# A graph network on one core: 340 stores of layer 0 issued from ScalarE's queue instead of SyncE's

## The chip, the core and the metric

The kernel runs on one NeuronCore of a Trainium2 chip. The core has TensorE (PE, matmuls; PEld are its weight loads), VectorE (DVE), ScalarE (ACT), GpSimd (POOL) and SyncE (SP). SP does no arithmetic here; it issues transfers. A transfer is an instruction in the queue of the engine that issues it, and 16 DMA engines then move the data. Each engine works its own queue in order, so an instruction that waits for a semaphore holds everything behind it on the same engine.

The metric is device time in microseconds for the whole program, one launch. Before the change it was 2840.71 us (median of three runs, 2832.33 to 2841.24).

## The reference

Two message-passing layers over a graph of 6250 nodes with 64 features and 206,250 edges sorted by target. Cut to what matters (LN is the layer norm):

```python
h = maximum(LN(x), 0)                                     # layer 0
msg = relu(h[src] + edge_attr_16 @ W_edge.T + b_edge)
h = (h + segment_sum(msg, dst)) @ W1.T + b1
x = x + relu(batch_norm(h)) @ W2.T + b2
h = maximum(LN(x), 0)                                     # layer 1
Y = relu(concat(h[src], edge_attr_64) @ M_W.T + M_b)
Z = segment_sum(Y, dst)
x = x + relu(concat(h, Z) @ U_W.T + U_b)
```

## The kernel before

**Groups and blocks.** Edges come in 101 groups of 16 tiles of 128 edges. The first 71 groups (targets of the low nodes) are sorted by their source's block: for each of 35 target blocks of 128 nodes the edges lie in a DRAM region `place` of 50 tiles, one tile for each source block and one for what overflows. DVE works out each edge's place (`places`, `rank`), POOL scatters the rows to `place` by 16 indirect transfers a group (L840), and SP fills the region with -1 beforehand (`fill_part`). The last 30 groups are not sorted: POOL gathers the source rows by indirect transfers (L545, class `Direct`).

**A step of a sorted block.** A block of 50 tiles is worked in seven steps of up to 8 tiles (`CH`, class `Sorted`). In layer 0 a step does this:

- `ahead` has SP load the block's rows `eb` (2050 KB, two buffers) and the next steps' source columns `st` (a row of DRAM `src_rows` spread over 128 partitions, six buffers). `columns`, once for each block, has PE transpose the column of sources, ACT writes it as `cols` (L331), and it is stored in `src_rows`; `sources` reads it back from there.
- `prepare`: PE transposes the 16 edge attributes, ACT copies them to `at` (L314), DVE compares `st` with the partition's number and so makes the 0/1 matrix `hot_s` (L434).
- `keep`: ACT casts `hot_s` to 8 bits, `hot_8` (L440, two buffers), and it is stored in DRAM `hots` for layer 1, which reads it in place of making it again.
- `gather`: PE multiplies `at` by the edge weights and `hot_s` by the node table's three parts `tab`; `messages`: ACT's relu to `msg` (L468); `targets`: DVE makes `hot_d` (L459); `sums`: PE multiplies `msg` by `hot_d` into the block's sum.

A `Direct` step of layer 0 makes the layer 1 edge terms as well: PE to `pe`, ACT copies them to `e1` (L611, two buffers), and they are stored in DRAM `terms`.

**What sets the order.** PE, DVE and ACT run in program order (`manual_schedule`). Every transfer that goes through the helper `load` (L139 to L142) is issued by SP and kept in program order, loads and stores alike: all have L141 in the profile. POOL's transfers are paced by `pace`: every other one waits for a matmul of the slot before. The two Line objects and `slot` interleave the steps of blocks with the sorting of later groups; a block's rows are loaded one slot before its `columns`.

**Semaphores of transfers.** In the built program the transfers of SP and ACT share eight completion semaphores, given out in turn in program order, and each transfer waits until the one eight places earlier has landed, unless its engine already knows that it has.

Of the kernel before, what the change touches and what calls it, by code (L numbers as in the profile page):

```python
# [37 lines left out]
F32 = mybir.dt.float32  # L38
# [8 lines left out]
P = 128  # L47
D = 64
# [31 lines left out]
def window(g):  # L80

    return min(max((g * GT * P * N // E - 31) // P, 0), SB - 2)
# [16 lines left out]
def gnn_kernel(  # L99
# [24 lines left out]
    nc = tc.nc  # L124
# [14 lines left out]
    def load(to, what):  # L139

        i = nc.sync.dma_start(to, what)  # L141
        return tc.keep_in_program_order(i) if in_order[0] else i  # L142
# [20 lines left out]
    def bank(shape, name, tag, bufs=1, dtype=F32):  # L163
        return ps.tile(shape, dtype, name=name, tag=tag, bufs=bufs)
# [157 lines left out]
    src_rows = dram.tile([SB, T * P], BF16, name="src_rows")  # L322
    hots = dram.tile([P, SB, T * P], F8, name="hots")

    def columns(layer, d, eb):

        if layer == 0:
            p = bank([T, P], "st_p", "tr")
            nc.tensor.transpose(p, eb[:, :, SRC], ident)
            cols = zero.tile([T, P], BF16, name="cols")  # L330
            nc.scalar.activation(cols, p, AF.Identity, bias=shift[:, d:d + 1])  # L331
            load(src_rows[d, :].rearrange("(t p) -> t p", p=P), cols)
        dl = work.tile([P, T, 1], F32, name="dl")
        nc.vector.tensor_scalar(dl[:, :, 0], eb[:, :, DST], float(-P * d), None, op0=OP.add)
        attrs = None
        if layer == 0:
            attrs = zero.tile([P, T, ED], F32, name="attrs")
            nc.scalar.copy(attrs, eb[:, :, D:D + ED])
        return dl, attrs
# [79 lines left out]
    class Sorted:  # L419
# [16 lines left out]
        def keep(self):  # L436

            n = self.n
            hot_8 = zero.tile([P, 8, P], F8, name="hot_8")
            nc.scalar.copy(hot_8[:, :n, :], self.hot_s[:, :n, :], saturate=False)  # L440
            load(hots[:, self.d, self.a * P:self.b * P],
                 hot_8[:, :n, :].rearrange("p t q -> p (t q)"))

        def gather(self):
            n, layer = self.n, self.layer
# [18 lines left out]
        def messages(self):  # L464
            n, gp = self.n, self.gp
            self.msg = msg = pools[self.layer].tile([P, 8, D], F32, name="msg", bufs=2 + self.layer)
            if self.layer == 0:
                nc.scalar.activation(msg[:, :n, :], gp[:, :n, :], AF.Relu)  # L468
            else:
                nc.vector.tensor_add(msg[:, :n, :], gp[:, :n, :], self.eb[:, self.a:self.b, 0:D])  # L470
                nc.scalar.activation(msg[:, :n, :], msg[:, :n, :], AF.Relu)  # L471
# [15 lines left out]
    class Blocks:  # L487
# [9 lines left out]
        def ahead(self):  # L497

            if self.i == len(self.list):
                return  # L500
            d, c = self.list[self.i]
            for b, from_c in ((d, 0), (d + 1, 1)):
                if b < SB and b not in self.rows and c >= from_c and self.age(b) >= 1:
                    self.rows[b] = self.load_rows(b)
            for b, from_c in ((d, 0), (d + 1, len(CH) - 1 if self.layer else 2)):
                if b in self.rows and b not in self.cols and c >= from_c and self.age(b) >= 2:
                    self.cols[b] = columns(self.layer, b, self.rows[b])
            there = self.rows if self.layer else self.cols
            for j in range(self.i, min(self.i + 6, len(self.list))):
                if j not in self.st and self.list[j][0] in there:  # L510
                    self.st[j] = sources(self.layer, *self.list[j])
# [39 lines left out]
    terms = dram.tile([ND, P, GT * D], F32, name="terms")  # L551
# [16 lines left out]
    class Direct:  # L568
# [30 lines left out]
        def messages(self):  # L599
            n = self.n  # L600
            half = slice(8 * self.h, 8 * self.h + n)
            if self.layer == 1:
                self.msg = self.gat[:, half, :]
                nc.vector.tensor_add(self.msg, self.msg, self.ea[:, half, :])
                nc.scalar.activation(self.msg, self.msg, AF.Relu)
                return
            self.msg = msg = zero.tile([P, 8, D], F32, name="msg")[:, :n, :]
            nc.vector.tensor_add(msg, self.pm[:, :n, :], self.gat[:, half, :])
            nc.scalar.activation(msg, msg, AF.Relu)
            e1 = self.pool.tile([P, 8, D], F32, name="e1", bufs=2)  # L610
            nc.scalar.copy(e1[:, :n, :], self.pe[:, :n, :])  # L611
            load(terms[self.g, :, 8 * self.h * D:(8 * self.h + n) * D],
                 e1[:, :n, :].rearrange("p t d -> p (t d)"))

        def sums(self):
# [77 lines left out]
    with tc.tile_pool(name="sort", bufs=1) as sort:  # L693
# [219 lines left out]
        for j0, j1 in chunks:  # L913
            n = j1 - j0
# [13 lines left out]
        with tc.manual_schedule(engines=ordered):  # L928
            for g in range(1, GS):
# [7 lines left out]
                d = window(g) + 3  # L937
# [34 lines left out]
    p = bank([P, P], "most_p", "tr")  # L972
# [69 lines left out]
    p = bank([P, P], "b2_p", "tr")  # L1042
# [59 lines left out]
    cols = [slice(a, min(a + 4 * P, NH * P)) for a in range(0, NH * P, 4 * P)]  # L1102
# [259 lines left out]
```

## Time and profile before

| what | value |
|---|---|
| median of three timed runs | 2840.71 us |
| profiled execution, its own time | 3512.69 us |
| span in the profile | 3510.9 us |
| mean granted TensorE clock | 0.767 |
| PE busy, share of the span | 63% |
| POOL busy | 59% |
| DVE busy | 48% |
| ACT busy | 24% |
| HBM moved | 538.24 MB, mean 153 GB/s |

The profiled execution took 3512.69 us, 24% over the median. Every duration and wait below is from that one execution, and a time worked out of it is brought to the timed runs by the factor 2840.71/3512.69 = 0.809, as a whole; the profile doesn't tell which of its stages were the longer for being recorded.

The stages can be told from where lines start and end: POOL's scatters (L840) run from 33 to 1817 us, its gathers for the last groups of layer 0 from 1823 us; the last `terms` store is issued at 2572 us; layer 1's first `st` load at 2632 us. In the rows of groups, a row gives line, engine, operation, tiles out<-in, count, then busy us and mean ns of one, then the engine's idle time just before these instructions and what ended most of it. "remote" there means a semaphore whose update the profile couldn't put down to an instruction. SPq and ACTq are the engines' queues; issuing a transfer isn't counted as busy.

### The profile page before, as it was taken

To read this page: it belongs to the slowest core of one execution; us is meant where nothing else is said; L and a number is where in the kernel's file an instruction comes from. 1 tells how busy PE (TensorE), PEld (TensorE's weight loads), DVE (VectorE), ACT (ScalarE), POOL (GpSimd) and SP (SyncE) were. 2 spreads that over 40 slices of the span, in tenths; PEclk is the share of its full clock that TensorE was granted. 3 is DMA by queue.
4 is the path that set the end of the run, shared out by engine and by line. 5 is a ranking of instruction groups with operands and counts; after the bars stand their busy time and mean duration, and the time that the engine had idled before them with its cause. 6 is when DMAs were issued, how large, how long until landed. Compare 5 with 4: busy or idle time off the path is not lost. (4 is left out here: it accounts for less than half of the span.)

```text
span 3510.9 us, 56266 instructions
## 1 busy us (share of the span) xinstructions
PE 2221.8 (63%) x20444; PEld 1666.0 (47%) x20444; DVE 1692.4 (48%) x3562; ACT 842.8 (24%) x1612; POOL 2060.9 (59%) x2098
## 2 busy tenths in 40 slices
PE   1336677677676766666675754444566767777777
PEld 1224455455454545444454533333345656565655
DVE  4725555455555545545442321121144656666667
ACT  1213233223233323223232210111131222222222
POOL 5666666666666666666665466666605455555552
PEclk7568877777778787778788876676677877878778
DMA  7747775766766776666644323232326545455553
GB/s 178 187 125 192 193 187 161 200 165 191 187 175 191 192 193 164 184 165 191 173 139 136 114 78 78 70 84 66 77 73 176 182 148 174 150 177 164 163 171 117
DMA packets 340180, 538.24 MB, mean 153 GB/s; under 512 B 114229, under 2 KB 245557, under 8 KB 330933
## 3 DMA queue, kind: packets, MB, share of 16 engines
q1 hardware_dynamic: 263972, 453.43, 45.5%
q0 software_dynamic: 66816, 79.02, 9.8%
q10 hardware_dynamic: 9104, 2.10, 0.4%
q8 instruction: 163, 2.67, 0.3%
q14 instruction: 125, 1.02, 0.1%
HBM read 358.81 MB, written 175.52 MB: 152 GB/s over the span
## 5 line engine op out<-in xcount | busy, mean ns | idle before, releaser
L840 POOL DMA_INDIRECT place<-to,ix x1136 | 1149.7, 1012 | 661.8 <-issue 284.2
L545 POOL DMA_INDIRECT gat<-table,src_d x952 | 903.2, 949 | 712.3 <-PE gp L148 213.7
L459 DVE TENSOR_TENSOR hot_d<-cbank,dl 128x1024 f32<-128x1024 f32 (+1 forms) x490 | 542.2, 1107 | 910.3 <-remote 332.5
L148 PE MATMUL pa<-hot_d,msg 128*64 128x128 f32 (+1 forms) x5250 | 859.0, 359 | 112.8 <-issue 91.6
L148 PEld LDWEIGHTS pa<-hot_d,msg 128*64 128x64 f32 (+1 forms) x5250 | 620.0, 182 | 237.1 <-issue 146.2
L148 PE MATMUL gp<-we,at 128*128 128x512 f32 (+1 forms) x490 | 290.9, 681 | 291.3 <-issue 167.8
L595 DVE TENSOR_TENSOR hot_d<-cbank,rel_d 128x1024 f32<-128x1024 f32 x120 | 145.7, 1214 | 504.7 <-remote 347.8
L148 PE MATMUL gp<-tab,st 128*128 128x64 bf16 x5250 | 258.4, 203 | 163.6 <-issue 146.1
L148 PEld LDWEIGHTS <-st 128*128 128x128 fp8e4 x5250 | 203.9, 104 | 235.4 <-issue 229.4
L148 PEld LDWEIGHTS <-hot_s 128*128 128x128 bf16 x5250 | 215.5, 106 | 182.9 <-issue 166.8
L471 ACT ACTIVATE msg<-msg 128x512 f32<-128x512 f32 (+1 forms) x245 | 143.0, 584 | 531.4 <-DVE msg L470 399.2
L314 ACT COPY at<-at_p 128x128 f32<-128x128 f32 (+1 forms) x245 | 64.9, 265 | 811.1 <-remote 478.3
L148 PE MATMUL gp<-tab,hot_s 128*128 128x64 bf16 x5250 | 229.5, 204 | 26.4 <-issue 21.8
L148 PEld LDWEIGHTS gp<-we,at 128*128 128x128 f32 (+1 forms) x490 | 90.9, 228 | 322.4 <-issue 184.1
L440 ACT CAST hot<-hot_s 128x1024 fp8e4<-128x1024 bf16 (+1 forms) x245 | 233.4, 953 | 43.2 <-DMA hots<-hot 18.9
L148 PE MATMUL pd<-hot_d,msg 128*128 128x256 f32 x476 | 149.8, 470 | 75.8 <-DVE acc L380 66.2
L470 DVE TENSOR_TENSOR msg<-gp,eb 128x512 f32<-128x512 f32 (+1 forms) x245 | 153.5, 627 | 90.9 <-remote 47.8
L148 PEld LDWEIGHTS pm<-we,ea 128*128 128x128 f32 x1136 | 175.6, 223 | 34.4 <-DMA ea<-in_ea 13.0
L148 PE MATMUL pm<-we,ea 128*128 128x128 f32 x1136 | 177.5, 307 | 20.8 <-DMA ea<-in_ea 13.1
L313 PE MATMUL at_p<-ident,attrs 128*128 128x128 f32 (+1 forms) x245 | 84.9, 347 | 140.8 <-issue 75.1
L148 PE MATMUL pe_d<-we,ea_d 128*128 128x128 f32 x476 | 85.3, 333 | 131.2 <-issue 60.5
L148 PEld LDWEIGHTS pe_d<-we,ea_d 128*128 128x128 f32 x476 | 78.2, 240 | 181.6 <-issue 94.7
(181 smaller groups left out, 2158.9 us busy)
## 6 DMA issues: line engine op xcount, KB each, us to landing
eb<-place SPq DMA_DIRECT2D x70, 2050.0 KB
place<-minus SPq DMA_DIRECT2D x175, 410.0 KB
st<-src_rows SPq DMA_DIRECT2D x210, 256.0 KB
ea<-in_ea SPq DMA_DIRECT2D x71, 512.0 KB
hots<-hot SPq DMA_DIRECT2D x210, 128.0 KB
st<-hots SPq DMA_DIRECT2D x210, 128.0 KB
place<-to,ix POOLq DMA_INDIRECT x1136
ea_d<-in_ea SPq DMA_DIRECT2D x30, 512.0 KB
```

The lines of the kernel that those rows point to most:

```text
L148: i = nc.tensor.matmul(*args, **kwargs)
L313: nc.tensor.transpose(p[:n * ED, :], attrs.rearrange("p t f -> p (t f)"), ident)
L314: nc.scalar.copy(at[:n * ED, :], p[:n * ED, :])
L440: nc.scalar.copy(hot_8[:, :n, :], self.hot_s[:, :n, :], saturate=False)
L459: nc.vector.tensor_tensor(self.hot_d[:, :n, :], slot_p[:, None, :].to_broadcast([P, n, P]), self.dl[:, self.a:self.b, :].to_broadcast([P, ...
L470: nc.vector.tensor_add(msg[:, :n, :], gp[:, :n, :], self.eb[:, self.a:self.b, 0:D])
L471: nc.scalar.activation(msg[:, :n, :], msg[:, :n, :], AF.Relu)
L545: i = nc.gpsimd.indirect_dma_start(out=gat[:, t, :], out_offset=None, in_=table, in_offset=bass.IndirectOffsetOnAxis(ap=src_d[:, k:k + 1], ...
L595: nc.vector.tensor_tensor(self.hot[:, :n, :], slot_p[:, None, :].to_broadcast([P, n, P]), rel_d[:, self.k:self.k + n, None].to_broadcast([ ...
L840: i = nc.gpsimd.indirect_dma_start(out=place[:, :], out_offset=bass.IndirectOffsetOnAxis(ap=ix[:, t:t + 1], axis=0), in_=to[:, t, :], in_o ...
```

## The change: three stores leave `load` for `nc.scalar.dma_start`

The stores of `cols` (35 of them, 12.5 KB each), `hot_8` (245, 128 KB each, 32 KB for a block's last) and `e1` (60, 256 KB, one of 128 KB) are issued by ACT, just behind the instruction that makes them. The 8-bit store is now described as 32-bit words, with the same bytes in each partition. Nothing else is edited.

```diff
@@ columns
-            load(src_rows[d, :].rearrange("(t p) -> t p", p=P), cols)
+            nc.scalar.dma_start(src_rows[d, :].rearrange("(t p) -> t p", p=P), cols)
@@ Sorted.keep
             nc.scalar.copy(hot_8[:, :n, :], self.hot_s[:, :n, :], saturate=False)
-            load(hots[:, self.d, self.a * P:self.b * P],
-                 hot_8[:, :n, :].rearrange("p t q -> p (t q)"))
+            nc.scalar.dma_start(hots[:, self.d, self.a * P:self.b * P].bitcast(F32),
+                                hot_8[:, :n, :].rearrange("p t q -> p (t q)").bitcast(F32))
@@ Direct.messages
             nc.scalar.copy(e1[:, :n, :], self.pe[:, :n, :])
-            load(terms[self.g, :, 8 * self.h * D:(8 * self.h + n) * D],
+            nc.scalar.dma_start(terms[self.g, :, 8 * self.h * D:(8 * self.h + n) * D],
                  e1[:, :n, :].rearrange("p t d -> p (t d)"))
```

In the built program PE's and POOL's order is the same as before, and DVE's but for two spots (one instruction some 60 places later, three neighbours exchanged). SP has 340 transfers fewer, ACT 340 more, each directly behind its L331, L440 or L611 and waiting for that instruction's end. 226 of the 340 also wait for the transfer eight places earlier to land; in 219 of these that one is SP's.

## The prediction, made before the changed kernel ran

> **What bounds the kernel now.** The waits of SP's own queue come first, since the change is about SP:
>
> ```profile
> SPq L141 <- ACT hot L440: 608.0, 114, 12.5
> SPq L141 <- ACT e L611: 206.5, 33, 26.3
> SPq L141 <- ACT cols L331: 84.9, 19, 44.0
> SPq L141 <- DMA src_rows<-cols: 39.5, 25, 3.3
> ```
>
> The columns are us in total, times, longest. SP stands 899 us (608.0 + 206.5 + 84.9) at the three stores, waiting for ACT to make what they store. The loads behind a store wait with it. Does anybody wait for those loads? The view of line L141 says who waited for its transfers:
>
> ```profile
> who waited for it (us, times):
>   DVE dl L334: 30.8, 4
>   POOL place L840: 29.4, 7
>   ACT hot L440: 24.0, 6
>   PE st_p L329: 16.3, 3
> ```
>
> Very little. Of POOL's 29.4 us, 26.3 are one wait at 33 us, before any of these stores. L334 and L329 wait for the same block rows `eb`, so they are one loss of 31 us. So SP isn't the bound. The windows by stage show what is:
>
> ```profile
> core 0: us, PE busy (x) PEld busy (x) DVE busy (x) ACT busy (x) POOL busy (x), PEclk, DMA share, GB/s
> 300.00:1800.00 1500.00, 1015.86 (x7603) 742.99 (x7601) 787.21 (x1953) 439.92 (x865) 961.49 (x952) 0.79 0.69 181
> 2000.00:2570.00 570.00, 288.88 (x1069) 202.56 (x1068) 120.63 (x178) 72.12 (x129) 357.50 (x378) 0.71 0.30 76
> ```
>
> From 300 to 1800 us, where 201 of the 245 `hots` stores lie, PE is busy 68% and POOL 64%, and POOL's row L840 has another 0.3 us of issue between transfers: PE and POOL together, coupled by `pace`, carry the stage. The DMA engines are at 69%, which at the timed run's length (69/0.81) would be near 85%, close enough to matter. ACT has 440 of 1500 us. From 2000 to 2570 us, where 53 of the 60 `terms` stores lie, POOL works its gathers at 358 us busy plus 0.3 us for each of 378, 83% of the stretch; ACT is busy 13%. Layer 1 holds none of the stores.
>
> **What is removed: SP's hold.** After the change the next thing that stops SP is the `st` load: in the program's list it waits for DVE's `hot_s`, which reads the buffer to be filled, one to three us before ACT's cast of the same step. So SP gets ahead by a few us, not freely. Worth of it, in the profile's time:
>
> - *Block rows.* DVE waits for `eb` four times, 30.8 us. In the timeline of SP's queue the last stop at a store ahead of those four loads is 1.0 us (store at 366.8), 3.8 (1461.1), 4.5 (1878.1) and 4.9 (1921.4). Loads can come earlier by that: 14 us.
> - *The store's own landing.* ACT's cast waits for the store two casts earlier to have left `hot_8`:
>
> ```profile
> 1461.13 0.33 SPq L141 DMA_DIRECT2D hots<-hot  x1
> 1461.51 1.57 SPq L141 DMA_DIRECT2D place<-minus  x1
> 1463.94 0.14 SPq L141 DMA_DIRECT2D eb<-place  x1
> ```
>
> ```profile
> 1476.82 1.04 ACT L440 CAST hot<-hot_s 128x1024 fp8e4<-128x1024 bf16 x1 [6.86 <-DMA hots<-hot]
> ```
>
> The 128 KB store issued at 1461.13 lets the cast go only at 1476.82, 15.7 us later, behind four fills of 410 KB issued from 1452.45 on. The Trainium skill ("DMA: Bandwidth & Descriptors", section on queues, rings and completion order) says that SP's and ACT's queues have rings of their own on each of the same DMA engines, which take turns between them. By that a store from ACT passes the fills; the trace has no ACT store to show it. Bounds: 0 (it lands no earlier) to 24.0 us (all waits of L440 for a landing). In two of the three places where these waits lie, `eb` lands at their end (386.5 and 1483.5) and holds DVE anyway, so I take half, 12 us.
> - *SP's wait for `src_rows`* (39.5 us) and 340 x 0.32 us of SP issue (the `hots` row of L141 has 320 ns as its middle): SP isn't on the path, 0.
>
> **What is added: ACT issues and waits.**
>
> - *Issue.* ACT's queue has issued transfers before, in the start-up:
>
> ```profile
> L916 ACTq DMA_DIRECT2D xc<-in_x x7: 347/404/657, 15.9 to 118.4; - x7
> ```
>
> These are least, middle and most ns. With 0.03 us from the cast's end to an issue (SP's stores follow L440 by that) I take 0.45 us for each, 340 x 0.45 = 153 us of ACT. Queued behind it on ACT are the copy of `pm` (L829), `attrs` and, above all, the next `at` (L314), for which PE's product waits. The timeline of a step:
>
> ```profile
> 923.78 1.05 ACT L440 CAST hot<-hot_s 128x1024 fp8e4<-128x1024 bf16 x1
> 924.71 0.44 ACT L824 COPY to<-raw 128x288 f32<-128x288 f32 x1
> 925.05 0.60 ACT L829 COPY to<-pm 128x512 f32<-128x512 f32 x1
> 928.47 0.27 ACT L314 COPY at<-at_p 128x128 f32<-128x128 f32 x1 [2.83 <-PE pa L148]
> ```
>
> ACT stands 2.8 us before L314, so PE's own work hides 0.45. By the view of `at`, L314 came after such an idle time 232 of 245 times (811.1/232 = 3.5 us on average); in the other 13 the issue is on the path, 13 x 0.45 = 6 us. For the 60 `terms` stores POOL's gathers are the cover: 0. If the cover were gone everywhere it would be the 153 us.
> - *The wait for the transfer eight places earlier.* This is new to ACT: in 219 stores it is a transfer of SP's. I compared, store by store, when that transfer was issued before with when the cast ended, and took the middle landing times that the trace's semaphore records give (7.1 us for a fill, 4.6 for `st`, 11.3 for `eb`). 20 stores would be late, by 40 us together, most behind a fill. The 3.5 us of idle time before L314 covers most of it: beyond 2.5 us each, 8 us are left. With all intervals at 0.81 it is 33 stores, 67 us, 18 beyond. Ends 0 and 67; I take 8.
> - PE, DVE and POOL: no instruction more or less.
>
> **Sum:** -14 - 12 + 6 + 8 = -12 us of 3512.7, times 0.809, -10 us. A little more lies in the DMA engines being kept fed in the stage where they are 69% busy; I round to -12 us: **2829 us**, 0.4% faster.
>
> **A rule against the change.** The same page, section "Issuing engines are not separate DMA queues", says that transfers from any engine run on the same 16 DMA engines and that issuing from several saves only the sequencer's time, usually small. By the rule the gain is 340 x 0.32 us of an SP that isn't the bound, nothing, and only the +14 us of ACT remain: 2840.7 + 11 = 2852. By the rows SP loses 899 us to order, which the rule doesn't count, but only some 26 us of that reach an engine. I follow the rows and keep 2852 inside the range.
>
> **Rivals.** Within 0.3% (about 8.5 us) can't be told from no change.
>
> - *ACT becomes tied to SP* (slower). At the timed run's shorter steps the 67 us of lateness isn't hidden, since PE is closer to always busy; then 67 + 6 against 26 gained is +47, times 0.809, **2879**. It decides once a store's wait passes the idle time before L314. For it: before, SP was never waited for by ACT but through `hot_8`; SP's transfer can itself stand behind an `eb` load or a fill. Against it: L314's 3.5 us, and the `hot_8` wait before asked for nearly the same, a landing some seven places back.
> - *Transfers bound the sorted stage in the timed run* (85%), and stops of SP leave them idle. Then 3% of the 1500 us come on top: -45 - 12 = -57, times 0.809, **2795**. For it: GB/s and the DMA share; against: nobody waits for loads in the profile.
> - *All of it hidden* or evened out: **2841**. For it: how few us wait on L141 at all.
> - *It doesn't free SP*: the `st` load stops SP at DVE in place of the store, at once. That also ends at 2841, or at 2852 with ACT's cost; it is counted in the two.
>
> **Chances:** 0.33 for 2829, 0.12 for 2795, 0.22 for no change, 0.28 for 2879, and 0.05 for slower in another way (ACT's issue slowed by SP's: one took 2.29 us at 17 us while SP issued fills). Faster 0.45, same 0.22, slower 0.33. The range, 2775 to 2885, reaches to both outer cases; the likeliest case's own is 2810 to 2838.
>
> **What would show it.** Right: SP's waits for L440, L611 and L331 gone and DVE's `hot_s` in their place; waits of L440 for `hots` near 0; DVE's L334 waiting under 20 us; the q10 queue with some 45 MB more and q1 as much less; ACT's issues near 0.4 us. Wrong: ACT waiting more than some 40 us at the three stores for SP's transfers, or PE's waits for L314 above their 122.7 us by more than some 20. A gain over 2% would mean that SP's hold reached PE or POOL by a path that the waits don't show.

## The result, and the profile after

The changed kernel takes 2856.29 us (median of eight runs, 2852.43 to 2863.96) against 2840.69 us before (eight runs, 2832.33 to 2844.32). The ratio is **1.0063**, with a 95% interval of 1.0051 to 1.0074: slower by 0.6%, where 0.4% faster was forecast. The range of the forecast holds the time, its direction is wrong.

One thing must be known to read the profiles: chips come in two kinds here. In the experiments below the kernel before takes 3501 to 3546 us in every execution on two chips, and 2821 to 2849 us on three others, a profiled one of 2840.61 us among them. So the 3512.69 us of the profile on which the prediction rests fit the first kind of chip and are not the price of recording, while the timed runs are from the second kind; all ratios here are between runs on one chip. The profile after has a span of 2850.7 us. The first experiment therefore profiles the kernel before on a chip of the second kind (span 2838.8 us), and it is this profile that the one after is held against.

The stops of SP's queue, before, on such a chip (us in total, times, longest):

```profile
SPq L141 <- ACT hot L440: 441.5, 155, 11.1
SPq L141 <- ACT e L611: 431.0, 58, 10.8
SPq L141 <- ACT cols L331: 127.4, 21, 8.9
```

and in the changed kernel:

```profile
SPq L141 <- PE pm_d L148: 429.2, 27, 19.3
SPq L141 <- DMA place<-to,ix: 418.5, 75, 20.1
SPq L141 <- DMA src_rows<-cols: 378.1, 34, 15.4
SPq L141 <- DVE hot_s L434: 107.4, 44, 6.8
```

The three stores are gone from it, but for one stop of 0.5 us. SP now stands elsewhere: at `eb`, which waits for POOL's scatters (271.5 us before), at `st`, which waits for `src_rows` to land (108.2) or for DVE's `hot_s` (5.4). In the unsorted groups the stop at `e1` (L611) is only exchanged for one at PE's `pm_d` (24.8 before), so nothing is freed there. Who waited for SP's transfers (us, times), in the changed kernel:

```profile
  ACT to L824: 63.7, 5
  DVE dl L334: 61.6, 8
  POOL place L840: 37.2, 20
  PE st_p L329: 27.7, 5
```

In the profile of before of 2838.8 us L334 has 76.0 us (11 times), L329 43.1 (8), L824 54.3 (6) and POOL's L840 28.5 (9). So the waits for block rows are 14 to 15 us shorter in total, the number that was forecast, while L824 and L840 wait 9 us longer each. None of the gain reaches the end. The sorted stage shows why; its windows, before:

```profile
core 0: us, PE busy (x) PEld busy (x) DVE busy (x) ACT busy (x) POOL busy (x), PEclk, DMA share, GB/s
300.00:1500.00 1200.00, 836.56 (x7208) 642.49 (x7207) 738.20 (x1838) 414.79 (x821) 911.91 (x896) 0.84 0.78 213
```

and after:

```profile
300.00:1500.00 1200.00, 811.91 (x7129) 625.98 (x7127) 732.78 (x1827) 419.08 (x811) 901.95 (x891) 0.84 0.77 211
```

POOL issues 896 scatters in 1200 us before, one each 1.34 us. A scatter that waits for nothing starts 1.28 us after the last (0.97 us busy, 0.30 us pause), so POOL works at 96% of what it can, at the same clock in both. **POOL is the bound of this stage** on such a chip, and in the changed kernel it gets five scatters less done. Its row, before (min/median/max ns, first and last start), and its stops for its own scatters (us, times):

```profile
L840 POOL DMA_INDIRECT place<-to,ix x1136: 964/972/1717, 33.1 to 1554.1; - x190
...
  DMA place<-to,ix: 50.2, 122
```

and after:

```profile
L840 POOL DMA_INDIRECT place<-to,ix x1136: 966/972/1758, 32.5 to 1563.8; - x190
...
  DMA place<-to,ix: 67.5, 151
...
  DMA place<-minus: 7.1, 7
```

The last scatter starts 9.7 us later, and the spans differ by 11.9 us. In all 13 traces from such chips 1279 to 1287 us pass between the last scatter and the end, so nearly all of the loss lies ahead of it. In the built program POOL's transfers have eight completion semaphores of their own (in the trace every scatter has the semaphore of the one eight places earlier), so a scatter waits until that one has landed: 8 x 1.28 = 10.2 us are allowed. With the 0.30 us of ordinary pause taken off each, POOL's stops for its scatters grow from 50.2 - 122 x 0.30 = 13.6 us to 67.5 - 151 x 0.30 = 22.2, and stops for fills add 7.1 - 7 x 0.30 = 5.0: together 13.6 us more. The other stops add 0.6 us, the scatters' own busy time is 3.9 us less, and the first scatter starts 0.6 us earlier; that makes the 9.7. Two such stops in the changed kernel, first what SP had issued, then POOL (in brackets idle time and what ended it):

```profile
499.40 3.72 SPq L141 DMA_DIRECT2D place<-minus  x4
...
505.37 1.17 SPq L141 DMA_DIRECT2D place<-minus  x1
```

```profile
510.62 0.97 POOL L840 DMA_INDIRECT place<-to,ix  x1 [0.30 <-issue]
513.08 0.97 POOL L840 DMA_INDIRECT place<-to,ix  x1 [1.49 <-DMA place<-to,ix]
516.03 0.97 POOL L840 DMA_INDIRECT place<-to,ix  x1 [1.98 <-DMA place<-to,ix]
```

Before, too, this slot has five fills in 6.8 us, and POOL stops behind them for 1.6 us over its pause, against 2.9 here. So fills in a row are not new; there are more of them. In the 10 us ahead of a scatter that lands over 10 us after its start (a late scatter; 88 of 1087 after, 44 of 1086 before), SP has issued 2.9 fills on average in the changed kernel, ahead of the others 0.9; of the loads `ea` it is 0.1 against 0.5.

SP's fills in another slot, in the timeline of its queue before, with two stores of `hots` and three loads of `st` left out between them:

```profile
974.67 0.43 SPq L141 DMA_DIRECT2D place<-minus  x1
...
976.35 0.88 SPq L141 DMA_DIRECT2D place<-minus  x1
...
980.23 0.53 SPq L141 DMA_DIRECT2D place<-minus  x1
...
982.47 0.37 SPq L141 DMA_DIRECT2D place<-minus  x1
```

and after, with only `st` loads left out:

```profile
969.41 0.43 SPq L141 DMA_DIRECT2D place<-minus  x1
...
970.39 1.02 SPq L141 DMA_DIRECT2D place<-minus  x1
...
974.60 0.37 SPq L141 DMA_DIRECT2D place<-minus  x1
...
975.64 0.67 SPq L141 DMA_DIRECT2D place<-minus  x1
```

Four fills of 410 KB each stand in 6.2 us instead of 7.8, and start as soon as `st` lets them. The `hots` stores between them had been **a metronome**: 155 of the 245 made SP wait for ACT's cast, and so spread the fills over ACT's steps. Of the 151 fills between 100 and 1550 us, 36 were close before, that is, issued within 2 us of the last one (from the end of one issue to the end of the next); 46 are after.

A second place where the profiles differ is on ACT. There the cast waits for its buffer, stands ahead of L871, and PE waits for that:

```profile
702.13 1.05 ACT L440 CAST hot<-hot_s 128x1024 fp8e4<-128x1024 bf16 x1 [2.22 <-DMA hots<-hot]
703.21 0.33 ACTq L441 DMA_DIRECT2D hots<-hot  x1
703.58 0.36 ACT L871 ACTIVATE acc<-u_p,b_c 64x128 f32<-64x128 f32 x1 [0.40 <-ACT hot L440]
```

PE's waits of `at_p` for L871 grow from 16.8 us (33 times) to 29.3. POOL's stops for PE grow by no more than 0.6 us over the stage, so in these two profiles little of it reaches POOL.

### The profile page after: what moved, and what is told of

It is laid out like the page before. It is cut to its first block, busy times and chain, and to the rows that moved or that the text cites. A ratio compares the mean times of both kernels' runs of the same rounds, so it can differ in the third digit from the quotient of the medians.

```text
span 2850.7 us, 56200 instructions
## 1 busy us (share of the span) xinstructions
PE 1946.8 (68%) x20444; PEld 1518.5 (53%) x20444; DVE 1668.7 (59%) x3562; ACT 850.0 (30%) x1612; POOL 2068.8 (73%) x2098
## 5 line engine op out<-in xcount | busy, mean ns | idle before, releaser
L840 POOL DMA_INDIRECT place<-to,ix x1136 | 1153.0, 1015 | 404.7 <-issue 244.9
L148 PE MATMUL pa<-hot_d,msg 128*64 128x128 f32 (+1 forms) x5250 | 700.7, 323 | 27.7 <-ACT msg L471 14.7
L148 PEld LDWEIGHTS pa<-hot_d,msg 128*64 128x64 f32 (+1 forms) x5250 | 537.5, 163 | 92.8 <-ACT msg L471 24.0
L148 PE MATMUL gp<-we,at 128*128 128x512 f32 (+1 forms) x490 | 270.6, 637 | 355.4 <-ACT at L314 355.4
L148 PEld LDWEIGHTS <-hot_s 128*128 128x128 bf16 x5250 | 205.8, 104 | 150.7 <-issue 125.5
L148 PEld LDWEIGHTS gp<-we,at 128*128 128x128 f32 (+1 forms) x490 | 85.4, 208 | 371.0 <-ACT at L314 364.1
L440 ACT CAST hot<-hot_s 128x1024 fp8e4<-128x1024 bf16 (+1 forms) x245 | 233.6, 953 | 146.3 <-DMA hots<-hot 83.4
L608 DVE TENSOR_TENSOR msg<-pm_d,gat 128x512 f32<-128x512 f32 (+1 forms) x60 | 41.2, 686 | 376.6 <-DMA gat<-table,src_d 376.5
L148 PE MATMUL pm_d<-we,ea_d 128*128 128x512 f32 x120 | 101.1, 938 | 194.8 <-DVE msg L608 194.8
L471 ACT ACTIVATE msg<-msg 128x512 f32<-128x512 f32 (+1 forms) x245 | 142.9, 584 | 298.9 <-DVE msg L470 286.5
L148 PE MATMUL gp<-tab,st 128*128 128x64 bf16 x5250 | 199.0, 195 | 39.9 <-DMA st<-hots 24.1
L148 PE MATMUL gp<-tab,hot_s 128*128 128x64 bf16 x5250 | 216.1, 201 | 1.5 <-DVE hot_s L434 1.5
L148 PEld LDWEIGHTS <-st 128*128 128x128 fp8e4 x5250 | 171.1, 99 | 83.7 <-issue 61.7
L824 ACT COPY to<-raw 128x288 f32<-128x288 f32 x71 | 30.8, 434 | 503.8 <-DMA place<-to,ix 436.0
L148 PEld LDWEIGHTS pm<-we,ea 128*128 128x128 f32 x1136 | 161.4, 209 | 18.7 <-DMA ea<-in_ea 12.2
L148 PE MATMUL pm<-we,ea 128*128 128x128 f32 x1136 | 163.0, 293 | 12.0 <-DMA ea<-in_ea 12.0
L609 ACT ACTIVATE msg<-msg 128x512 f32<-128x512 f32 (+1 forms) x60 | 37.6, 626 | 395.1 <-DVE msg L608 394.6
L148 PEld LDWEIGHTS pm_d<-we,ea_d 128*128 128x128 f32 x120 | 25.3, 255 | 214.8 <-DVE msg L608 214.1
```

The lines of the kernel that those rows point to most:

```text
L148: i = nc.tensor.matmul(*args, **kwargs)
L824: nc.scalar.copy(to[:, :, D:RW], raw)
L840: i = nc.gpsimd.indirect_dma_start(out=place[:, :], out_offset=bass.IndirectOffsetOnAxis(ap=ix[:, t:t + 1], axis=0), in_=to[:, t, :], in_o ...
```

## The experiments

Four theories were put to the test. A: the time that ACT spends issuing stores costs. B, called H later on: SP, freed of its stop at the cast, issues loads and fills closer together, and they delay POOL's scatters. C: the cast's wait for its own store's landing costs. R: the stores, as a third queue at the DMA engines, take turns with POOL's transfers and delay them, whatever SP does.

**Before, unchanged, and each part alone** (one chip, kernel before 2837.51 us):

> The kernel before, unchanged. It gives what the first profile could not, a trace whose length is that of the timed runs. All theories: a span near 2839 us and a ratio of 1.000 (+-0.001). Stage ends to be compared with the changed kernel's (end of the sorting scatters near 1500 us, last edge-term store near 2170 us, layer 1 from 2226 us). Theory A (ACT's time at the issue): the 15.6 us lie in the sorted stage, ACT's casts L440 wait for the landing of hots about as long as after (83 us), PE's wait for the at of L314 is some 15 us shorter than 355. Theory B (SP no longer held lets loads and fills collide with POOL's scatters): POOL's place transfers and the waits of L824 for them are shorter than after by 10 us or more, SP's hold at L440 is again hundreds of us. Theory C (the store's own landing): L440 waits clearly less than 83 us for hots.

> Only the 35 stores of cols go to ACT's queue. Theory A: 35 x 0.4 us, few of them on the path: ratio 0.999 to 1.002. Theory B: SP no longer stands at L331 but still at L440, so nearly all of the loss is absent: within 1.000 +-0.002. If it is this part that costs (the st loads waiting for src_rows 378 us on SP), 1.004 to 1.006.

> Only the 245 stores of the 8-bit matrices go to ACT's queue. Theory A: 245 x 0.33 to 0.40 us of ACT, some 15% of it on the path of PE: nearly the whole loss, ratio 1.004 to 1.007. Theory B: also the whole loss, since these stores were SP's longest hold: 1.004 to 1.007, with POOL's scatters later. Theory C: the same, with L440 waiting for hots above 60 us. If the loss is spread over the parts: 1.002.

> Only the 60 stores of edge terms go to ACT's queue, in the stage that POOL's gathers bound. All three theories: nothing, 0.999 to 1.001. If these stores share in the loss (256 KB each from ACT's queue competing with the gathers), 1.002 to 1.004, with the direct stage longer by 6 to 12 us.

Each of the last three has one of the three hunks of the change (`cols`, the 8-bit `hots`, `terms`). Measured: before against itself 1.0008 (1.0001 to 1.0015), so differences of 0.1% are not read here; `cols` 0.9992 (0.9982 to 1.0002); `hots` **1.0065** (1.0052 to 1.0078); `terms` 1.0006 (0.9994 to 1.0018). The whole loss is in the 8-bit stores, and it lies ahead of the last scatter: with them on ACT it starts 18.3 us later than before, and the span is 17.6 us longer. C falls in its simple form: before has 105.1 us of L440's waits for `hots`, more than the 64.2 us of the slower kernel. A isn't settled here: PE's wait for L314 is 348.8 us before, 355.4 with the whole change, but 371.1 with the 8-bit stores alone, and how much of that comes from POOL being late isn't told apart.

**Four kernels to part A, R, H and C** (one chip, before 2829.8 us). `e4_sp_late` leaves the stores with SP, one step later (cut; those left over are issued behind the loop):

```diff
-            hot_8 = zero.tile([P, 8, P], F8, name="hot_8")
+            hot_8 = zero.tile([P, 8, P], F8, name="hot_8", bufs=3)
...
-            load(hots[...], hot_8[...])
+            while owed:
+                owed.pop()()
+            owed.append(lambda: load(hots[...], hot_8[...]))
```

> The stores of the 8-bit matrices stay on SP's queue, but each is issued one step later, where the next one stood, with a third hot_8 buffer: SP is freed of its hold for ACT's cast (441 us in the clean trace of before), ACT issues nothing, and no second hardware queue carries data. What is at stake: POOL's scatters that land over 10 us after their issue (44 of 1086 before, 108 with the hots stores on ACT) and POOL's waits for its own scatters (50 against 78 us). Theory R (a third queue takes turns with POOL's scatters at the DMA engines): as before, ratio 0.998 to 1.002, some 45 late scatters. Theory H (SP's hold had spaced its fills and loads; freed, they bunch and delay the scatters): 1.004 to 1.007, some 90 to 110 late scatters. Theory A (ACT's time at the issue): as before, 1.000.

`e5_act_held` has them on ACT, and SP's next transfer waits for the cast:

```diff
         i = nc.sync.dma_start(to, what)
+        while owed:
+            tc.add_manual_dep(i.ins, owed.pop(), SYNC, reason="held until the cast")
...
-            nc.scalar.copy(hot_8[...], self.hot_s[...], saturate=False)
-            load(hots[...], hot_8[...])
+            cast = nc.scalar.copy(hot_8[...], self.hot_s[...], saturate=False)
+            nc.scalar.dma_start(hots[...].bitcast(F32), hot_8[...].bitcast(F32))
+            owed.append(cast.ins.name)
```

> The stores of the 8-bit matrices are on ACT's queue, and SP's next transfer waits for the cast all the same, so SP stands where it stood before. Theory R: the loss stays, 1.005 to 1.007, some 100 late scatters. Theory H: the loss goes, 0.999 to 1.002, some 45 late scatters, POOL's waits for its scatters near 50 us. Theory A: the loss stays, 1.005 to 1.007, with few late scatters.

`e6_act_dummy` is the kernel before with a spare copy on ACT (0.36 us in the middle; its edit stands below), and `e7_act_bufs3` has the stores on ACT with `bufs=3`:

```diff
             load(hots[...], hot_8[...])
+            spare = zero.tile([P, 192], BF16, name="spare", bufs=1)
+            nc.scalar.copy(spare, self.hot_s[:, :2, :].rearrange("p t q -> p (t q)")[:, :192])
```

> The kernel before, with a copy of 192 columns (some 0.33 us) added on ACT behind each of the 245 casts, where the issue of a store stands in the changed kernel; all transfers as before. Theory A: most of the loss, 1.004 to 1.007. Theories R and H: nothing or a few us, 0.999 to 1.002.

> The stores of the 8-bit matrices on ACT's queue, with three hot_8 buffers in place of two, so that a cast waits for the store three casts earlier. L440's waits for hots (64 us in the two-buffer run) fall under 15 us in any case. Theory C (the cast's wait for its own store's landing carries the loss): 0.999 to 1.002. Theories R, H and A: the loss stays, 1.004 to 1.007, since what decides is POOL's queue.

Measured: e4 0.9985 (0.9975 to 0.9995), e5 **0.9999** (0.9988 to 1.0010), e6 1.0004 (0.9994 to 1.0013), e7 1.0027 (1.0019 to 1.0035). In e5 every `hots` byte leaves by ACT's queue, described as 32-bit words, and ACT issues 245 times; yet the loss is gone. So R and A fall, the new description isn't the cause either, and e6 says the same of A. What e5 put back is SP's stop (the line numbers are shifted by three):

```profile
SPq L141 <- ACT hot L443: 648.2, 125, 12.7
```

e4 was the miss of H: it predicted a loss and 90 to 110 late scatters, and there is no loss, with 15 of them. SP isn't free there. It still stands 367.8 us at the casts, one step behind, and 32 fills are close. So it seems that a stop one step late spaces the transfers well enough; this was read from the trace, not foretold. In e7 the waits of L440 for `hots` are out of ACT's list of waits and `at_p` waits 15.0 us for L871, but 60 fills are close and a loss stays, though less than H's 1.004. Either the cast's wait carries the missing part, or this chip loses less: the two-buffer kernel wasn't run on it, so this stays open.

**Which transfers had to be spaced.** The next four make SP wait for the latest cast at all transfers, at the fills alone, at the inputs `raw` alone, or not at all. They ran on a chip of 3520 us (before 3523.37):

> The whole change, all three stores on ACT's queue, with SP's next transfer made to wait for the cast as before. Theory H (SP freed of its stop at the cast bunches its transfers, POOL's scatters land late and stop POOL): 0.999 to 1.001, late scatters (over 10 us) down from 88 to 20 to 45. If moving cols or terms as well undoes this: 1.003 to 1.006.

> The 8-bit stores on ACT's queue; only the fills of place (410 KB each, 113 of them) wait for the latest cast, everything else of SP only behind them in the queue. If it is the fills that have to be spaced: 0.999 to 1.001. If it is the group's inputs raw and ea, whose landing went from some 5 to some 10 us: 1.004 to 1.006. If any of SP's bytes in a bunch do it, between: 1.001 to 1.003.

> The 8-bit stores on ACT's queue; only the group's inputs raw (and ea behind them) wait for the latest cast. If it is the fills that have to be spaced: 1.003 to 1.006, since of four fills a group three have no inputs before them. If it is the inputs: 0.999 to 1.001.

> The 8-bit stores on ACT's queue once more, on the chip of the three others, as their measure: theory H 1.004 to 1.007. If the third buffer of the earlier run took part of the loss away, this lies clearly above its 1.0027; if the chips differ in the loss, it lies at 1.002 to 1.004.

Measured, in this order: 1.0015 (1.0002 to 1.0028), 1.0019 (1.0006 to 1.0033), 1.0001 (0.9990 to 1.0012) and 0.9999 (0.9982 to 1.0016). The last is the kernel that loses 0.65% elsewhere; here it loses nothing. POOL's row of e11, with what ended its idle time:

```profile
L840 POOL DMA_INDIRECT place<-to,ix x1136: 964/972/1759, 31.2 to 1812.4; - x190
...
  remote: 93.3, 65
  PE gp L148: 87.5, 74
  PE rk L148: 50.1, 19
```

A scatter comes every (1812.4 - 31.2)/1135 = 1.57 us, not 1.34: `pace` holds POOL back for PE, and its scatters have time to land. Here 56 of 155 fills are close (36 of 156 in the first profile of before), but only 22 of 1024 scatters are late, against 52 of 996. So on such a chip close fills don't make scatters late in the first place.

The same four kernels on a chip of 2838.59 us:

> Only the 8-bit stores on ACT's queue, once more. On a chip where the kernel before takes some 2840 us POOL issues its scatters almost without a pause (1.28 us each), and late scatters stop it: 1.004 to 1.007, POOL's own stops for its scatters some 15 us above the kernel before. On a chip of 3520 us TensorE holds POOL back and the loss is hidden: 0.998 to 1.002.

> The whole change with SP's next transfer waiting for the cast. Theory H on a chip of 2840 us: 0.999 to 1.001, well under the run with the 8-bit stores alone. If moving cols or terms costs too: 1.003 to 1.006.

> The 8-bit stores on ACT's queue, only the fills wait for the latest cast. On a chip of 2840 us: 0.999 to 1.001 if the fills are what has to be spaced; 1.004 to 1.006 if the inputs are; 1.001 to 1.003 if each has a share.

> The 8-bit stores on ACT's queue, only raw and what stands behind it wait for the latest cast. On a chip of 2840 us: 1.003 to 1.006 if the fills are what has to be spaced, 0.999 to 1.001 if the inputs are.

The holds of the last two are the dependency above, on the latest cast, put on the fills alone (113 of the 175 get it) or on `raw` alone. The edit for the fills:

```diff
         i = load(to[:, a:a + PART, :], minus[...])
+        if owed:
+            tc.add_manual_dep(i.ins, owed[0], SYNC, reason="held until the cast")
```

Measured: `hots` stores alone **1.0071** (1.0055 to 1.0088); the whole change held **0.9997** (0.9988 to 1.0006); fills held **0.9987** (0.9980 to 0.9995); inputs held 1.0039 (1.0025 to 1.0052). With the hold the whole change loses nothing, and for the 8-bit stores holding the fills alone is enough. POOL's view of the kernel with the 8-bit stores alone, and then with the fills held:

```profile
L840 POOL DMA_INDIRECT place<-to,ix x1136: 968/972/2280, 32.1 to 1565.3; - x190
...
  DMA place<-to,ix: 65.9, 154
```

```profile
L844 POOL DMA_INDIRECT place<-to,ix x1136: 966/972/1747, 34.3 to 1554.6; - x190
...
  DMA place<-to,ix: 49.4, 129
```

But SP's queue is in order, so a held fill holds what stands behind it too. Told by the number of scatters that POOL had started, at 1.34 us each, the kernel with the 8-bit stores alone issues the fills 8.6 us earlier than e0 on average, and `raw` 11.9. With the fills held it is 0.8 and 5.5, with `raw` held 5.2 and 1.1. So each hold moves both, and the hold on `raw`, which leaves the fills early, takes back some of the loss as well (1.0039 against 1.0071). The fills weigh most, but how much of it the inputs carry isn't separated.

The last two were on a chip of 3520 us again (before 3523.07):

> The whole change, three hot_8 buffers, and the fills alone held until the latest cast. Theory H on a chip of 2840 us: 0.997 to 0.999, faster than before by the waits of L440 and what the freed inputs and columns gain; scatters that land after more than 10 us near 40 or fewer. If the stores on ACT have a cost of their own that the hold only hid: 1.000 to 1.003. On a chip of 3520 us 0.998 to 1.002.

> The kernel before, all stores on SP's queue; of the four fills of a slot the first and second are moved back and the fourth forward, so that up to four stand in a row (1640 KB). Theory H, by the fills alone, on a chip of 2840 us: 1.003 to 1.010, over 80 scatters that land after more than 10 us. If bunched fills are not enough by themselves: 0.999 to 1.002. On a chip of 3520 us: 0.998 to 1.003.

`h1_best` is the whole change with three buffers and the fills held; `h2_fills_burst` is the kernel before with the four `fill_part()` of a slot in one place. They gave 1.0008 (0.9990 to 1.0026) and 1.0018 (1.0001 to 1.0035), too little to tell either from no change; `h2_fills_burst` has 90 close fills of 156 there, and 32 late scatters of 1002. Whether close fills alone are enough for the loss, and whether h1 gains, stays open on a chip of 2840 us. The best that was measured there are e4 and g3, at 0.9985 and 0.9987, only little beyond what before against itself shows.

All runs on chips of about 2840 us, with counts from the traces: close fills (of 151), late scatters (of some 1087 from 100 us on; landing is the last record of their semaphore before its next use), POOL's stops for them over 0.30 us each, and `at_p`'s wait for L871.

| kernel | before on that chip, us | ratio | close fills | late scatters | POOL's stops, us | at_p, us |
|---|---|---|---|---|---|---|
| before (e0) | 2837.5 | 1.0008 | 36 | 44 | 13.6 | 16.8 |
| cols (e1) | 2837.5 | 0.9992 | 33 | 59 | 17.9 | 18.6 |
| terms (e3) | 2837.5 | 1.0006 | 31 | 40 | 12.8 | 15.5 |
| hots (e2) | 2837.5 | 1.0065 | 57 | 108 | 32.0 | 25.2 |
| after | 2840.7 | 1.0063 | 46 | 88 | 22.2 | 29.3 |
| SP, one step late (e4) | 2829.8 | 0.9985 | 32 | 15 | 4.0 | 15.0 |
| hots, SP held (e5) | 2829.8 | 0.9999 | 37 | 28 | 9.5 | 15.0 |
| spare copy (e6) | 2829.8 | 1.0004 | 34 | 24 | 7.5 | 15.0 |
| hots, 3 buffers (e7) | 2829.8 | 1.0027 | 60 | 46 | 12.7 | 15.0 |
| hots (g1) | 2838.6 | 1.0071 | 56 | 101 | 19.7 | 28.8 |
| all, SP held (g2) | 2838.6 | 0.9997 | 41 | 54 | 17.2 | 16.8 |
| hots, fills held (g3) | 2838.6 | 0.9987 | 37 | 39 | 10.7 | 15.2 |
| hots, inputs held (g4) | 2838.6 | 1.0039 | 57 | 79 | 20.8 | 25.9 |

Within each group with one chip the kernels that lose have the most close fills and the most late scatters. Over the whole table close fills part it in two: up to 41, no loss; from 46, a loss. But this cut was found after the runs and is narrow: counted from start to start instead, e4 has 44 and after 49. Late scatters part it as well, at most 59 against at least 79, but for e7. The trace columns are of one execution each, and e7's took 2830.5 us, less than its median of 2837.12, so its late scatters and stops are rather too few.

## Why the prediction was wrong

- **What bounds the kernel.** "PE and POOL together" was read from a profile in which POOL was busy 64% of the stage. The step that brought every wait "as a whole" by 0.809 to the timed runs hid that at their length POOL has hardly any slack: 1.34 us for each scatter where 1.28 is the least. In the first profile it was 1.57. The 3512 us fit the other kind of chip, where the waits are longer and the single instructions are not, so one common factor can't bring them over. That DMA engines near 85% would be "close enough to matter" was near the cause (78% measured), and the rival built on it had the sign the wrong way round: it had the engines starve, not crowd.
- **SP's hold.** Right in what happens: the stops at the stores vanish and `hot_s` takes part of their place. **The step that failed is "Worth of it":** it asked only who waits for SP's transfers and counted each earlier one as a gain. It put at nothing what transfers that come closer together do to POOL's scatters. The profiles show 13.6 us more of POOL's stops for that, where the sum had -12 us in all, and g3 shows that it is the loss: with the fills held the ratio falls from 1.0071 to 0.9987.
- **Block rows, -14 us.** Measured -14.4 (L334) and -15.4 (L329), and worth nothing, since POOL's queue sets the stage. That the number agrees is luck: it was 14 of 30.8 us on the one kind of chip, and is 14.4 of 76.0 on the other, and the forecast's own mark, L334 under 20 us, is missed with 61.6.
- **The store's own landing, -12 us.** L440's waits fell by 21.7 us, from 105.1 to 83.4, not to near 0. A store of 128 KB landed 5.3 us after its issue in the middle, 5.5 before, so little is seen of its passing the fills. And 40 casts wait in place of 31, some ahead of L871, where PE's waits grew by 12.5 us. The total got better and the place worse.
- **ACT's issue, +6 us.** An issue of `hots` took 326 ns in the middle, and e6 and e5 find no cost that can be told from none. PE's waits for L314, at 355.4 us far over the forecast's 122.7, are 348.8 in the kernel before on that kind of chip, so this mark said nothing.
- **The wait for the transfer eight places earlier, +8 us.** 4 `hots` stores of 245 came over 1 us after their cast, 18.5 us together. Small, as forecast; the same rule on POOL's own eight semaphores, which the prediction didn't look at, is where the loss lies.
- **The rule against the change** came out nearest with 2852, but by luck: its loss is a cost on ACT that the runs don't find. SP's issue time was indeed worth nothing. What the rule leaves out is that the queue's order also paced the transfers.
- **The other rivals.** ACT tied to SP (2879): its mark, over 40 us of waiting at the stores, isn't there (20 us). Transfers bound (2795) and hidden (2841): no, on these chips; on a chip of 3520 us, hidden it was. What came true is "slower in another way", by a way that the 0.05 didn't name. That SP isn't freed is true of the unsorted groups, where stops of 431.0 us became 429.2.

## What to carry to other kernels

A wait that nobody seems to wait for can be what spaces the transfers behind it. Before taking it away, look for the transfer that will move up and for the engine whose own transfers then land later, above all one that works without a pause and waits for its n-th last transfer. If the stop goes, keep the spacing: a dependency on the bulky transfers, and by the queue's order on what stands behind them, was enough here. And hold a profile's span against the timed runs first: a stall in a longer execution can be the slack that hides the cost in the shorter.

## What the runs showed of the hardware

The same kernel takes 2830 to 2840 us (medians) on three chips and 3523 us on two others, at a mean granted clock of 0.84 and 0.77. The clock is 9% apart, the time 24%. The middle durations of single instructions are the same on both: a scatter 972 ns, a cast L440 1046 ns, a matmul of L148 242 ns. So it is mostly waits that are longer; why, isn't explained here. The 8-bit stores on ACT cost 0.65% on the one kind and nothing that shows (0.9982 to 1.0016) on the other.

An indirect scatter on POOL follows the last one after 1.28 us at the least, and with eight semaphores has 10.2 us to land before POOL stops for it. In the kernel before 44 of 1086 took over 10 us, with the 8-bit stores on ACT 108 of 1087.
